# Two graph layers on one core: vectors by TensorE, four banks for the first preparation, later casts, chains cut at their bank, an earlier verdict

## The chip, the cores and the metric

The kernel runs on one core of a Trainium2 chip. Its time is the device time of the whole launch in microseconds (us). The engines of the core are called TensorE (PE in the profile; PEld is its weight load), VectorE (DVE), ScalarE (ACT), GpSimd (POOL) and SyncE (SP). Each executes its own stream of instructions in order, and they wait for each other through semaphores. Transfers between DRAM and on-chip memory are issued by SP, ACT or POOL.

## The reference

The input is x, 16 graphs (batches) of 1024 nodes with 256 features in float32, and adj, 16 matrices of 1024 x 1024 integers that are 0 or 1. Two layers follow each other. Layer 0 has 4 heads of 64 features and one edge type that occurs:

```python
h = einsum('bnd,hde->bhne', x, W)
e_src, e_dst = einsum('bhne,hte->bhtn', h, a_src), einsum('bhne,hte->bhtn', h, a_dst)
weight = where(adj == 0, -1e9, leaky_relu(mask * (e_src[i] + e_dst[j]), 0.01))
dst = softmax(weight) @ h + bias
out = norm_per_head(relu(dst) + h) * ln_gamma + ln_beta
x = layernorm(x + out)
```

Layer 1 is a transformer block with 8 heads of 32 features, whose queries, keys and values are all the normed input, and whose logits are masked by adj:

```python
normed = layer_norm(x, gamma1, beta1)
x1 = x + softmax(mask(q @ q.T / sqrt(32))) @ q        # q: normed, by heads
y = layer_norm(x1, gamma2, beta2)
x = layernorm(x + x1 + gelu(y @ W1 + b1) @ W2 + b2)
```

## The kernel before

`fast_path` holds the whole computation for the inputs that it assumes, and writes what it found about them into a small tile; `tile_two_graph_layers` makes one number, the verdict, from it, loads it into a register on all engines, and branches to a slow `general_path` where it is 0. With these inputs it is 1.

**Two streams in one program.** `layer0()` and `layer1()` are Python generators. Each yields after a piece of TensorE work, with the size of the piece and the tiles that the next one needs. A planner loop at the end of `fast_path` chooses which stream goes on. Layer 1 of batch b runs beside layer 0 of batch b+1. The planner keeps `place`, how far each stream is, and `COURSE`, which says how far layer 0 should be for each position of layer 1; `SLACK`, `SLACK1` and `STAY` say by how much the order may deviate, and `WORK0`, `WORK1` and `ATTN1` are the sizes of a batch in units of about 1 us of TensorE. The class `Pace` models the times that the engines need. The resulting order is the order of the instructions on TensorE, VectorE, ScalarE and GpSimd. SP is left to the framework, which may issue SP's transfers earlier than they are written.

**Chains.** Small work behind the matmuls (norms, residuals, copies) is a chain: a generator begun with `begin(chain, engine, *needs)` and driven on by `advance()` when the model finds its needs met. A chain is recorded as a user of the tiles that it needs or makes. When a buffer is to be reused, `settle` or `bank0` first runs its users to their end (`complete`), waits for other engines included.

**PSUM.** Of 8 banks, `ps_s` holds four (named ps: logits and hidden layer), `ps_o` two (po), and `ps_a` two (acc0 and acc1), handed out by `bank0` for layer 0 and for transposes.

**The front.** Layer 0's matrix W is loaded into `w0e` by eight transfers on ACT. `w0e` has eight more columns, W times a_src and a_dst for each head. For them a_src and a_dst are broadcast to all 128 partitions (four loads of 320 KB, two on SP and two on ACT), multiplied with W on VectorE and summed. `later_weights` is a chain that loads the vectors of the norms and the biases, and layer 1's w1 and w2 (1 MB each), on SP, and later folds gamma2 into w1 and beta2 into b1 (16 matmuls into po, w_sb<-w_sb,g_c on VectorE). `prepare` makes for each pair of 128-row blocks: xT (transposes through acc, copied by ScalarE), the projection acc<-w0e,xT, the exponentials dinv and v0 of the scores, hb (h), and `mask`. In batch 0 the mask comes from adjacency blocks ak, cast to bf16 by a POOL transfer and turned by TensorE; in later batches from adjb, a copy of adj cast to bf16 in DRAM (`cast_adj`, two POOL transfers a batch), read back through transposing transfers on SP (`load_adj`). `turn_sources` writes the exponentials of e_src to DRAM (esr<-rows), and `spread_factor` reads them back broadcast to all partitions (cb<-esr, 512 KB for each half of the rows and pair of heads; four groups a batch).

**Layer 0's attention** (`attention0`, 32 steps a batch) makes two weight tiles a step on VectorE (p<-cb,dinv,mask) three steps ahead, and multiplies them with v0 on TensorE (acc<-v,p). `residual0` and `after0` follow for each head or pair of heads: norm per head, sum with x (tile xl), layer 1's first norm, its transposed result nT for keys and queries (acc<-ident,sq, or ps), the values v1 and the input x1 of the residual. `handed` passes these to layer 1; when `half` asks for one that is not there, `finish_norms` completes the whole chains.

**Layer 1.** `attention1` has 32 steps a batch (half of the queries, four heads, block of 128 keys): four logits ps<-nT, their exponentials on ScalarE (p<-ps), the mask on VectorE (p<-p,mask), and the products into po in two shapes. Then `finish1` (residual and norm), and `mlp` in four chunks (ps<-yT,w_sb; gelu to hid on ScalarE; po<-w_sb,hid). `last_norm` adds the residual and writes zz and then out. `in_range` compares the collected sums (`seen`) of a batch with bounds and keeps the minimum in okr.

Of the kernel before, what the change touches and what calls it, by code (L numbers as in the profile page):

```python
# [39 lines left out]
P = 128  # L40
# [150 lines left out]
def fast_path(  # L191
# [19 lines left out]
    ok: bass.AP,  # L211
# [67 lines left out]

    w0e = const.tile([P, DC, D + 2 * H0], F32, name="w0e")  # L280
    for c in range(DC):
        for h in range(H0):
            nc.scalar.dma_start(w0e[:, c, h * HO : (h + 1) * HO], w0[h, c * P : (c + 1) * P, :])
# [4 lines left out]
    terms = ((a_src, nc.sync, w0e[:, :, D + H0 : D + 2 * H0]), (a_dst, nc.scalar, w0e[:, :, D : D + H0]))  # L288

    at = one.tile([P, 3, PAIR, HO, T], F32, name="v0")  # L290
    vectors = [at[:, i, :, :, :] for i in range(3)] + [one.tile([P, PAIR, HO, T], F32, name="xl")]
    for i, (src, queue, _) in enumerate(terms):
        for pair in range(H0 // PAIR):
            queue.dma_start(
                vectors[i * PAIR + pair].rearrange("p h e t -> p (h e t)"),
                bass.AP(
                    tensor=src.tensor,
                    offset=src.offset + pair * PAIR * HO * T,
                    ap=[[0, P], [1, PAIR * HO * T]],
                ),  # L300
            )

# [6 lines left out]
    for i, (_, _, dst) in enumerate(terms):  # L309
        for c in range(DC):  # L310
            t = two.tile([P, H0, HO], F32, name="z")
            for pair in range(H0 // PAIR):
                heads = slice(pair * PAIR, (pair + 1) * PAIR)
                nc.vector.tensor_mul(
                    t[:, heads, :],
                    w0e[:, c, pair * P : (pair + 1) * P].rearrange("p (h e) -> p h e", e=HO),
                    vectors[i * PAIR + pair][:, :, :, 0],
                )
            nc.vector.tensor_reduce(dst[:, c, :], t, axis=mybir.AxisListType.X, op=OP.add)
# [12 lines left out]
    def later_weights():  # L332
        for t, src in ((lng0_r, lng0), (lnb0_r, lnb0), (g1_r, gamma1), (be1_r, beta1), (b2_r, b2)):
            nc.sync.dma_start(t, bass.AP(tensor=src.tensor, offset=src.offset, ap=[[0, P], [1, D]]))
        for t, src in ((g1_c, gamma1), (be1_c, beta1), (g2_c, gamma2), (be2_c, beta2)):
            nc.sync.dma_start(t, src.rearrange("(c p) -> p c", p=P))
        nc.sync.dma_start(b1_sb, b1.rearrange("c p -> p c"))
# [4 lines left out]
        nc.sync.dma_start(w1_sb, w1.rearrange("(c p) f -> p c f", p=P))  # L342
        nc.sync.dma_start(w2_sb, w2.rearrange("(c p) d -> p c d", p=P))
# [16 lines left out]
        for c in range(DC):  # L360
            nc.vector.tensor_scalar(w1_sb[:, c, :], w1_sb[:, c, :], g2_c[:, c : c + 1], None, op0=OP.mult)
# [54 lines left out]
    def transpose_rows(dst, src, scale=None, shift=None):  # L416

        pt = side_bank([P, DC, GB, P])
# [74 lines left out]
    def load_x(t, b, k, count):  # L493
        nc.sync.dma_start(t, x[b, k * P : (k + count) * P, :].rearrange("(g p) d -> p g d", p=P))

    adj_blocks = {}
    x_blocks = {}
# [24 lines left out]
    def load_blocks(i):  # L522
        b, k = divmod(i, NB // GB)
        if b < B:
# [3 lines left out]
    def prepare(b, hb, esr, cbs, v0, dinv, mask):  # L528
# [4 lines left out]
        def turn_mask(k):  # L533
            i = b * NB + k
            pt = adj_blocks.pop(i)
            if b == 0:
                ak = pt
                pt, _ = bank0([P, NB, P], BF16)
# [15 lines left out]
            load_adj(i + 3)  # L554

        turning, scaling = [], []
        if b:
            cast_adj(b + 1)
        for k in range(0, NB, GB):
# [4 lines left out]
            transpose_rows(xT, xk)  # L564
            yield 0.45, bank0_ready, xT
            if b == 0:
                turn_mask(k)
                yield 0.0, bank0_ready, xT
# [4 lines left out]
            for g in range(GB):  # L573
# [4 lines left out]
                ph, bank = bank0([P, D + 2 * H0])  # L578
# [15 lines left out]
                yield 0.45, bank0_ready  # L594
                if g == 0 and b == 0:
                    if k == BPH:
                        cast_adj(1)
# [979 lines left out]
```

## Time and profile before

| What | us |
|---|---|
| median of 3 runs (lowest, highest) | 3255.43 (3252.06, 3255.72) |
| the profiled execution's own time | 3255.19 |
| its span, from first to last instruction | 3253.4 |
| TensorE busy | 3168.4 (97%) |
| VectorE busy | 2882.5 (89%) |
| ScalarE busy | 1961.9 (60%) |
| GpSimd busy | 511.3 (16%) |
| mean granted TensorE clock | 0.992 |

The profile is of one execution. An instruction's line tells the engine, the operation and its tiles as out<-in; numbers in the names are left out, so that a_src's vectors, v0 and v1 all read as "v", and w1, w2 as "w_sb". The operations are all recorded at one line of the file, the helper `Engine.call` (L61), so they are told apart by their tiles. A "q" behind an engine's name means its sequencer, which issues transfers and waits. "issue" in a chain is time for which the profile shows no wait. An idle time tells what ended it. Idle time of an engine that others do not wait for costs nothing.

### The profile page before, as it was taken

The numbers are of one execution on the slowest core, as the hardware profiler recorded it, in microseconds if no ns is written. First come the engines' busy times: TensorE is split into PE (matmuls) and PEld (weight loads), VectorE is DVE, ScalarE is ACT, GpSimd is POOL, SyncE is SP. The second block draws the span as 40 slices with busy tenths as digits, with TensorE's granted clock in tenths as the row PEclk, the third lists the DMA queues.
The fourth block names the chain that finished last, engine by engine and source line by source line (L and its number), as shares of the span: only waits on it lengthen the run. The fifth ranks groups of instructions, "written<-read, shape, count | busy, mean of one in ns | idle before, by whom it ended". The sixth has DMA issues, their size and how long they took to land.

```text
span 3253.4 us, 147229 instructions
## 1 busy us (share of the span) xinstructions
PE 3168.4 (97%) x67297; PEld 1979.3 (61%) x67297; DVE 2882.5 (89%) x4943; ACT 1961.9 (60%) x4256; POOL 511.3 (16%) x462
## 2 busy tenths in 40 slices
PE   5899999999999999999999999999999999999998
PEld 4557565575756657566575755757566575665745
DVE  5899898998989989898998989989898998989992
ACT  2473846748376583856738466483755838567483
POOL 1202112030110202112030120301102021120300
PEclk9799999999999999999999999999999999999999
DMA  7212202122031221303122031220312213011000
GB/s 169 58 38 59 63 26 67 39 63 52 26 85 21 70 46 32 87 20 73 36 66 56 26 74 33 63 52 25 87 26 68 41 42 80 20 44 21 30 7 16
DMA packets 209447, 163.18 MB, mean 50 GB/s; under 512 B 138480, under 2 KB 189680, under 8 KB 207856
## 3 DMA queue, kind: packets, MB, share of 16 engines
q1 hardware_dynamic: 204640, 119.07, 14.8%
q0 software_dynamic: 2592, 33.56, 5.3%
q8 instruction: 529, 8.67, 1.1%
q10 hardware_dynamic: 1584, 1.05, 0.1%
q14 instruction: 102, 0.84, 0.1%
HBM read 138.68 MB, written 48.50 MB: 58 GB/s over the span
## 4 chain that ended last, share of the span: by engine, by line
PE 75%; DVE 16%; ACT 4%; issue 3%; DMA 1%; POOL 0%; ACTq 0%; SPq 0%; POOLq 0%; DVEq 0%
PE po L61 28%; PE ps L61 28%; PE acc L61 19%; DVE p L61 14%; ACT p L61 2%; ACT o L61 0%; ACT nT L61 0%; DMA cb<-esr 0%; DVE o L61 0%; DVE st L61 0%; ACT zz L61 0%; DVE v L61 0%; DVE hb L61 0%; DVE z L61 0%; DVE relu L61 0%
## 5 line engine op out<-in xcount | busy, mean ns | idle before, releaser
L61 DVE TENSOR_TENSOR p<-p,mask 128x1024 f32<-128x1024 f32 x1024 | 1191.2, 1220 | 6.9 <-ACT p L61 6.9
L61 ACT ACTIVATE p<-ps 128x512 f32<-128x512 f32 x2006 | 1042.4, 612 | 235.9 <-PE ps L61 220.0
L61 DVE SCALAR_TENSOR_TENSOR p<-cb,dinv,mask 128x512 f32<-128x512 f32 x1024 | 709.3, 747 | 8.1 <-DMA cb<-esr 7.8
L61 PE MATMUL ps<-nT 32*128 32x512 f32 x4012 | 647.1, 641 | 2.2 <-ACT p L61 0.4
L61 ACT ACTIVATE hid<-ps,b_sb 128x256 f32<-128x256 f32 x512 | 242.0, 474 | 586.1 <-PE ps L61 586.1
L61 PE MATMUL acc<-v,p 128*64 128x65 f32 x16384 | 563.5, 225 | 31.0 <-DVE p L61 21.9
L61 PEld LDWEIGHTS po<-v,p 128*32 128x32 f32 x32768 | 397.3, 109 | 315.7 <-issue 264.6
L61 PEld LDWEIGHTS acc<-v,p 128*64 128x64 f32 x16384 | 536.7, 140 | 75.1 <-issue 14.4
L61 PE MATMUL po<-p,v 128*32 128x512 f32 x2048 | 543.4, 605 | 1.3 <-DVE p L61 1.3
L61 PE MATMUL po<-p,unit 128*32 128x512 f32 x2048 | 543.5, 605 | 0.0
L61 PE MATMUL po<-w_sb,hid 128*64 128x256 f32 x4096 | 476.2, 380 | 0.0
L61 PE MATMUL ps<-yT,w_sb 128*64 128x256 f32 x4096 | 475.7, 380 | 0.0
L61 POOL TENSOR_SCALAR r<-mv 128x4 f32<-128x4 f32 (+1 forms) x128 | 86.5, 676 | 2057.4 <-DVE mv L61 2019.5
L61 PE MATMUL po<-v,p 128*32 128x33 f32 x32768 | 393.1, 198 | 7.2 <-issue 6.7
L61 PEld LDWEIGHTS po<-w_sb,hid 128*64 128x64 f32 x4096 | 281.3, 137 | 146.3 <-issue 14.5
L61 PEld LDWEIGHTS ps<-yT,w_sb 128*64 128x64 f32 x4096 | 283.6, 137 | 135.4 <-issue 5.2
L61 POOL TENSOR_TENSOR r<-r,mhalf 128x8 f32<-128x8 f32 (+2 forms) x192 | 313.6, 1633 | 16.0
L61 PEld LDWEIGHTS ps<-nT 32*128 32x128 f32 x4012 | 201.9, 183 | 131.7 <-ACT p L61 84.5
L61 PEld LDWEIGHTS po<-p,v 128*32 128x32 f32 x2048 | 77.8, 108 | 321.7 <-issue 143.4
L61 DVE TENSOR_TENSOR z<-hb,bias_r 128x256 f32<-128x256 f32 x128 | 54.2, 423 | 163.8 <-ACT hb L61 163.8
L61 PE MATMUL acc<-w0e,xT 128*128 128x264 f32 x512 | 174.5, 435 | 10.5 <-issue 10.5
L61 ACT ACTIVATE mask<-ak,shift_c 128x1024 uint8<-128x1024 bf16 x120 | 142.1, 1184 | 0.0
(115 smaller groups left out, 2437.7 us busy)
## 6 DMA issues: line engine op xcount, KB each, us to landing
cb<-esr SPq DMA_DIRECT2D x64, 512.0 KB
adjb<-in_adj_dram POOLq DMA_DIRECT2D x30, 1024.0 KB, 11.5
xk<-in_x_dram SPq DMA_DIRECT2D x64, 256.0 KB
xl<-in_x_dram SPq DMA_DIRECT2D x32, 512.0 KB
out_dram<-zz SPq DMA_DIRECT2D x64, 256.0 KB
ak<-adjb SPq DMA_TRANSPOSE x240
ak<-in_adj_dram POOLq DMA_DIRECT2D x8, 256.0 KB, 6.8
w_sb<-in_L_gnn_W_dram SPq DMA_DIRECT2D x2, 1024.0 KB
```

Of the source, the lines that this page charges most:

```text
L61: return method(*args, **kwargs)
```

## The change

In the front:

- x's first block is the first transfer on SP. a_src and a_dst are loaded as one row of 5 KB each, on one partition. A matmul with a row of ones (taken from okr, which is set to 1) spreads each over 128 partitions in a ps bank, and VectorE multiplies whole 256-column rows of W with it. W comes in two transfers.
- `later_weights` issues its transfers on ACT instead of SP. The scaling of w1 by gamma2 goes from VectorE to ScalarE.
- batch 0's preparation takes its banks from the four of ps instead of the two of acc (`front_bank`).
- batch 1's casts are issued at the third step of batch 0's attention, no longer in its preparation, and its first three adjacency blocks are read at the 21st step.

In the rounds:

- `after0` ends with nT. The values (`values1`) and x1 with its ratio (`rows1`) are chains of their own; `half` completes only the chain that makes nT, and `values` asks for v1 when the products need it.
- `last_norm` ends with its sum out of po; the norm behind it is the chain `norm_rows`.
- b2 is added 70 instead of 60 us (in the model's time) after its half. `WORK0`, `SLACK1`, `STAY` and `COURSE` get other values.

At the end: the comparison of the last batch's sums, and a new `judge` that reduces everything to the verdict (with a transpose through a ps bank), stand ahead of the last chunk of the last batch's MLP. The steps behind the last norm that did so before, with an identity matrix of their own, go.

```diff
+    x_blocks = {0: two.tile([P, GB, D], F32, name="xk")}
+    load_x(x_blocks[0], 0, 0, GB)
+    terms = one.tile([P, H0, HO, T], F32, name="v0")
+    for i, src in enumerate((a_src, a_dst)):
+        nc.sync.dma_start(
+            terms[i * Q : i * Q + 1].rearrange("p h e t -> p (h e t)"),
+            bass.AP(tensor=src.tensor, offset=src.offset, ap=[[0, 1], [1, H0 * HO * T]]),
+        )
...
-        for h in range(H0):
-            nc.scalar.dma_start(w0e[:, c, h * HO : (h + 1) * HO], w0[h, c * P : (c + 1) * P, :])
+        nc.scalar.dma_start(
+            w0e[:, c, 0:D].rearrange("p (h e) -> p h e", e=HO),
+            w0[:, c * P : (c + 1) * P, :].rearrange("h p e -> p h e"),
+        )
...
+    for i, at in enumerate((D + H0, D)):
+        spread = ps_s.tile([P, D], F32, name="ps")
+        nc.tensor.matmul(
+            spread, okr[i * Q : i * Q + 1, 0:P], terms[i * Q : i * Q + 1, :, :, 0], start=True, stop=True
+        )
         for c in range(DC):
             t = two.tile([P, H0, HO], F32, name="z")
+            nc.vector.tensor_mul(t.rearrange("p h e -> p (h e)"), w0e[:, c, 0:D], spread)
+            nc.vector.tensor_reduce(w0e[:, c, at : at + H0], t, axis=mybir.AxisListType.X, op=OP.add)
...
-        nc.sync.dma_start(w1_sb, w1.rearrange("(c p) f -> p c f", p=P))
-        nc.sync.dma_start(w2_sb, w2.rearrange("(c p) d -> p c d", p=P))
+        nc.scalar.dma_start(w1_sb, w1.rearrange("(c p) f -> p c f", p=P))
+        nc.scalar.dma_start(w2_sb, w2.rearrange("(c p) d -> p c d", p=P))
...
-            nc.vector.tensor_scalar(w1_sb[:, c, :], w1_sb[:, c, :], g2_c[:, c : c + 1], None, op0=OP.mult)
+            nc.scalar.activation(w1_sb[:, c, :], w1_sb[:, c, :], AF.Copy, scale=g2_c[:, c : c + 1])
...
+    def front_bank(b, shape):
+        return bank0(shape) if b else (ps_s.tile(shape, F32, name="ps"), {})
...
-            load_adj(i + 3)
+            if b or k + 3 < NB:
+                load_adj(i + 3)
...
+            if b == 0 and i == 2:
+                cast_adj(1)
+            if b == 0 and i == 20:
+                for k in range(3):
+                    load_adj(NB + k)
...
-        yield "vector", normed
+        handed[b, n] = [None, None, nT]
+        norms[b, n, "values"] = values1(b, n, normed)
+        begin(norms[b, n, "values"], "vector", normed)
+        norms[b, n, "rows"] = rows1(b, n, normed, v2, r2, r3)
+        begin(norms[b, n, "rows"], "vector", normed, r3)
...
+    def values1(b, n, normed):
         v1 = two.tile([P, BPH, H1, HD + 1], F32, name="v1")
...
+        handed[b, n][1] = v1
+        yield from ()
+
+    def rows1(b, n, normed, v2, r2, r3):
         ratio = small.tile([P, BPH], F32, name="ratio")
...
+    def judge():
+
+        right = small.tile([P, NR], F32, name="seen")
+        nc.vector.tensor_scalar(right[:, : B * NB], types, N / 2 + 2.0, None, op0=OP.is_lt)
+        nc.vector.tensor_tensor(okr[:, : B * NB], okr[:, : B * NB], right[:, : B * NB], op=OP.min)
+        least = const.tile([P, 1], F32, name="least_r")
+        nc.vector.tensor_reduce(least, okr, axis=mybir.AxisListType.X, op=OP.min)
+        row = side_bank([1, P])
+        nc.tensor.transpose(row, least, ident)
+        nc.vector.tensor_reduce(least[0:1, :], row, axis=mybir.AxisListType.X, op=OP.min)
+        nc.vector.tensor_copy(verdict, least[0:1, :])
...
+            if b == B - 1 and (n, q) == chunks[-1]:
+                in_range(seen)
+                judge()
...
-        if g < GB - 1:
-            return
+        if g == GB - 1:
+            begin(norm_rows(b, k, z, mv), "vector", z)
...
-                    finish_norms(b, n)
+                    complete(norms[b, n, H0 - 1])
...
-    WORK0 = NB // GB * 2.25 + 2.0 + NB * H0 * 1.0
+    WORK0 = NB // GB * 2.0 + 2.0 + NB * H0 * 1.0
...
-    SLACK1 = 0.02
-    STAY = 0.017
-    COURSE = [(0.0, 1.0), (REST1 + 1.0, 1.0), (ATTN1, 1.31), (WORK1 - 12.0, 2.0), (WORK1, 2.0)]
+    SLACK1 = 0.03
+    STAY = 0.01
+    COURSE = [(0.0, 1.0), (REST1 + 1.0, 1.0), (ATTN1, 1.29), (WORK1 - 10.0, 2.0), (WORK1, 2.0)]
```

## The prediction

> **What bounds the kernel now.** I read the table of the engines first, then the kernel cut into windows, then the chain that ended last for both ends, then the waits and the order of time where the chain leaves TensorE (PE).
>
> ```profile
> PE 3168.4 (97%) x67297; PEld 1979.3 (61%) x67297; DVE 2882.5 (89%) x4943; ACT 1961.9 (60%) x4256; POOL 511.3 (16%) x462
> ```
>
> TensorE is busy for 3168.4 of 3253.4 us, so whoever moves nothing but waits can win 85 us at most. The windows (window: length, then busy PE, PEld, VectorE (DVE), ScalarE (ACT), POOL; granted clock; DMA share; GB/s) tell where these lie:
>
> ```profile
> 0.00:20.00 20.00, 1.94 (x12) 1.64 (x12) 3.61 (x16) 2.98 (x4) 3.10 (x10) 1.00 0.87 197
> 20.00:40.00 20.00, 16.23 (x105) 11.78 (x106) 7.42 (x19) 13.69 (x47) 3.12 (x6) 1.00 1.08 276
> 40.00:60.00 20.00, 10.01 (x227) 9.24 (x227) 11.09 (x20) 1.68 (x7) 0.00 (x0) 0.74 0.81 160
> 60.00:80.00 20.00, 14.39 (x349) 11.71 (x346) 19.79 (x36) 0.63 (x1) 1.93 (x2) 1.00 0.16 55
> ...
> 480.00:500.00 20.00, 20.00 (x392) 16.15 (x389) 19.69 (x46) 6.99 (x15) 3.89 (x4) 1.00 0.10 29
> ```
>
> Until 50 us no computing engine is full, while the 16 DMA engines nearly are (shares 0.87, 1.08, 0.81): the front waits for transfers. From 50 to 98 VectorE sets the pace (19.79 of 20), because batch 0's layer 0 runs with no layer 1 beside it. From 144 us on TensorE is full (20.00 of 20), with VectorE close behind (19.69). Over 200 to 3000 us all windows together show PE 2782 of 2800 busy. Layer 0's weights end at 120.7 in batch 0 and at 3072.7 in batch 15, so a round takes (3072.7 - 120.7)/15 = 196.8 us, of which about 1.3 are idle. So the two ends can be shortened, and the fifteen rounds between can hardly gain, but can lose fifteen times over.
>
> The chain of the front (start, length, what):
>
> ```profile
> 1.23 5.24 DMA v<-in_L_gnn_a_src_dram
> 6.47 0.02 issue
> 6.49 8.04 DMA w0e<-in_L_gnn_W_dram
> 14.53 0.02 issue
> 14.55 0.33 ACTq L61
> ...
> 20.89 4.66 PE acc L61 x16
> ...
> 32.16 3.78 DMA esr<-rows
> 35.94 0.02 issue
> 35.95 14.15 DMA cb<-esr
> 50.11 0.02 issue
> 50.13 1.47 DVE p L61 x3
> ```
>
> An old load holds a new one: ScalarE's queue cannot issue a load before an unrelated older one has landed, and ScalarE starts computing only at 14.9, behind its last issue. The first projection (20.89) waits for the columns made from a_dst, landed at 19.95. At the end the 14.15 us of cb stand alone: it shares the DMA engines with batch 1's two casts (issued at 33.3) and with w1 and w2 (2 MB, issued at 21.0).
>
> **The front, part by part.** (1) Vectors. Four broadcasts of 320 KB become two loads of 5 KB on one partition, behind x on SP: issues at 0.8, 1.2 and 1.7 (about 0.45 us each). The nearest row for their landing is esr<-rows, also small, 3.78 us: they are there at 5.9. W in two loads instead of eight, the same 256 KB: from 6 us (one issue and the latency of that row) to 14.5 (as now). The early transfers sum to about 2.2 MB by the profile's sizes (two x, W, three ak, bias, and 0.5 MB of xl, whose tile is now free at once); at the 197 to 276 GB/s of the rows that is 8 to 11 us, W is in the middle, I take 9.5. Then VectorE does four products of 128x256 and four reductions; three pairs follow the last half of W: 3 x (0.42 + 0.42) = 2.5 us, so the projection starts at 12.0 instead of 20.89. The product now reads PSUM. [...] here relu<-acc from PSUM takes 425 ns and hb<-hb,relu from SBUF 424, so I add nothing. The two spread matmuls (at most 0.44 us each, as acc<-w0e,xT with 264 columns) end before W lands.
>
> (2) Four PSUM banks instead of two for batch 0's preparation. From projection to second esr write: 32.16 - 20.89 = 11.3. ScalarE is busy 13.69 of the 16.8 us from 23.2 to 40, so the ping-pong costs at most 3 us over three to four blocks; I take 1.0 off the two blocks on the path (0 to 1.8): 22.3. esr lands as now, 3.8 later: 26.1.
>
> (3) cb without casts, w1 and w2. Bounds: 5 us (1 MB at the 211 GB/s of 0 to 60 us) and 14.15. Only the last ak blocks and x are beside it: 6.5, so the first p at 32.6. The rest of preparation ends at 12.0 + (42.3 - 20.9) - 2 = 31.4, inside. **Gain 50.1 - 32.6 = 17.5**, between 12 and 22. [...] But SP's order is free here (it issues w1 at 21 us, though it is written behind batch 0's preparation), while ScalarE's is the written one: the bytes leave the window. I take the row.
>
> What moves to later must hide. **Casts** (4 MB read) start after two steps of attention, about 36 us, and land within 12 us or so each (median 11.5); batch 1's masks are first made at 126.2, now about 109: 50 us of cover. They run beside the cb of group 2, whose buffer is free after eight steps and which is needed after sixteen; a step takes (98 - 50.1)/26 = 1.84 us there (52 p in that window, two to a step), so 15 us of cover against at most the 14 of now: I take 0, at most 3. **ScalarE's ten small loads** stand before the squares of the first head pair (10 x 0.35 us and waits for older landings); ScalarE is busy 0.63 of 20 us there. Behind them wait the squares, and for these VectorE; it takes the first (v0s) at 77.3 now, 27 us after its first p. w1 and w2 (issued at step 14, 32.6 + 14 x 1.84 = 58, some 10 us of transfer) are wanted by the matmuls that stand at 99.24 now, about 82 after. SP loses twelve issues. The three adjacency blocks queue their six transposing loads on SP at step 20, no longer ahead of esr; before, they blocked SP from 43.9 to 56.
>
> **Handoff to layer 1, 98 to 144.** VectorE, the pace-setter, loses the two scalings of w1 (1.41 us, to ScalarE, idle for 16.7 us there) from its path. The values, ratio and x1 of the first half (116.0 to 119.3, 3.3 us) stand before the last two p now; as own chains they may come later. I count half: 1.4 + 1.6 = **3.0 us**, between 0 and 5.
>
> **Rounds.** The course asks for 0.29 x 42 = 12.2 units of layer 0 by the end of attention 1, not 0.31 x 43 = 13.3. So about one step moves from attention 1 (where each insertion changes the array's shape) into the MLP phase (same 128x64 shape). Nearest price: the four logits of ps<-nT from a shape change take some 0.1 to 0.2 us longer than their work, so two half steps are 0.3 us; chains that stop at their bank and no longer hold VectorE for POOL (t<-r waits 23.5 us in all) can take some of the 1.3 idle. Against that, layer 0 ends two units later (about 1.6 us each by 76 us for 49 units). I take -0.27 a round, **4 us in 15 rounds**, from -15 to +10 in all.
>
> **Tail.** The last matmul ends at 3239.8, then:
>
> ```profile
> 3242.32 0.16 DVE t L61
> 3242.48 0.15 DVE right L61
> ...
> 3245.11 0.14 DVE verdict L1537
> ```
>
> After it all engines load the verdict (0.5 us) and branch; ScalarE is back 2.9 us after its branch, TensorE 4.6, and the span ends 2.9 us after TensorE. With the verdict long there, TensorE branches at 3240.3 and is back by 3245.0, ScalarE (last work to 3243.7) is back by 3247.1, and the end comes at 3250.0 to 3250.5: **3.0 us**, between 0 (if the last store sets the end) and 3.4. The price: in_range and judge (about 1.9 us of VectorE) now stand before a transpose ahead of the last chunk's matmuls on TensorE; VectorE is busy 4.5 of 20 us there but comes from a norm: 0 to 2.5, I take **0.6 lost**.
>
> Sum: 17.5 + 3.0 + 4.0 + 3.0 - 0.6 = 26.9 us. The profiled execution took 3255.2 (1.8 outside its span), the median is 3255.4: **3228 us**.
>
> **Rivals.** (A) The rounds gain too: the whole idle of 1.3 us and 0.3 of shape changes go, 15 x 1.6 = 24 instead of 4: 3208. For it: stalls by "DVE relu" and "DVE p" recur; against: TensorE and VectorE are both full. (B) The front gains little: cb stays slow ([...]7.7 us), and the casts and w1, w2 then collide with the second cb and ScalarE's queue (5 us): 3241. (C) Slower: the later end of layer 0. Each round's last norm chain then hands the second half's keys 3.2 us late, and the fifth step of attention 1 needs them: in round 2 the last p ends at 507.9, keys are stored from 530.9, the fifth logits start at 534.6. The slack is about 2.6 us there; planner's fillings may not cover it. If every round loses L, the end is 3232 + 15 L: it decides against the change above L = 1.6; at 2.2 it gives 3265. (D) The front's and the handoff's gain are given back in the VectorE stretch, where a load moved there (cb of group 2, or w1 for the matmuls at 99.24) comes that much late: 3228 + 20.5 + 3 = 3252.
>
> **Chances.** Main 0.60 (own range 3217 to 3239), A 0.12, B 0.16, C 0.07, D 0.05. Within 0.2% (6.5 us, about what a measurement of this kernel tells from no change) of 3255.4 fall most of D and a little of C: 0.04. Slower: 0.05. Faster: 0.91. The range from 3211 to 3246 leaves out C and D, and half of A at the lower end.
>
> **What the changed profile would show.** First projection near 12 and first p near 33 (wrong: above 40); cb landing in 5 to 8 us; attention windows still VectorE-full; last mask of batch 15 about 24 us earlier; a round between 196.2 and 197.2 (C: over 198.4, with TensorE waiting for nT or sq just after each MLP); 10.5 us from last matmul to end, not 13.6. A ScalarE queue that stands on its issues while VectorE waits for the squares would make the front's sum wrong.

## The result, and the profile after

The changed kernel takes 3212.38 us (median; 3207.75 to 3217.06), beside 3255.57 for the kernel before on the same chip (3252.06 to 3256.20): a ratio of 0.9868, 95% interval 0.9852 to 0.9883. The gain of 43 us is larger than the 27 forecast, inside the range (3211 to 3246) by 1.4 us, and it comes from other places than forecast. The profiled execution took 3212.37, its span is 3210.5 (before 3253.4).

From the page of the changed kernel, busy time, share of the span and instructions of each engine:

```profile
PE 3145.5 (98%) x67301; PEld 1966.0 (61%) x67301; DVE 2876.0 (90%) x4936; ACT 1964.8 (61%) x4258; POOL 498.0 (16%) x460
```

TensorE's busy time fell from 3168.4 to 3145.5 us, with practically the same number of matmuls. Over half of the gain was therefore counted as busy time before, and a bound of the rounds that is read from idle time misses it.

Where the 42.9 us of span lie can be read from four marks in both traces: the first weight tile p of batch 0, the first gelu (hid) of batch 0's MLP, the first gelu of batch 15's, and the end. (A "round" is the time from a batch's first gelu to the next one's. Where a mean round is given below, it is that of the fourteen from batch 0 to batch 14: 197.2 us before, 195.1 after. The fifteenth has no layer 0 beside it and takes 177.4 and 177.6.)

| stretch (us) | before | after | difference | forecast |
|---|---|---|---|---|
| start to first p | 50.1 | 39.3 | -10.8 | -17.5 |
| first p to first gelu of batch 0 | 195.8 | 197.0 | +1.2 | -3.0 |
| from there to first gelu of batch 15 (15 rounds) | 2938.7 | 2909.4 | -29.3 | -4.0 |
| from there to the end | 68.8 | 64.7 | -4.0 | -3.0 + 0.6 |

**The front.** The windows of the changed kernel (window: length, then busy PE, PEld, DVE, ACT, POOL; granted clock; DMA share; GB/s):

```profile
0.00:20.00 20.00, 12.26 (x78) 9.47 (x79) 7.36 (x24) 10.19 (x30) 5.37 (x15) 1.00 0.85 180
20.00:40.00 20.00, 6.20 (x47) 4.50 (x45) 4.17 (x10) 7.32 (x28) 0.80 (x2) 0.75 1.05 228
40.00:60.00 20.00, 16.40 (x398) 14.47 (x399) 19.83 (x35) 0.63 (x1) 0.00 (x0) 0.91 0.55 83
60.00:80.00 20.00, 14.96 (x336) 13.02 (x334) 19.76 (x36) 0.63 (x1) 2.62 (x2) 0.86 0.38 133
```

VectorE is full from 40 us on (before, its first weight tile came at 50.1). But between 20 and 40 the DMA engines are as full as before (1.05), and no computing engine is busy for more than 7.32 of the 20 us. The chain of the changed kernel says what they wait for:

```profile
1.45 8.44 DMA ak<-in_adj_dram
9.89 0.05 issue
9.94 2.92 PE ps L61 x12
...
20.81 8.73 DMA esr<-rows
29.54 0.02 issue
29.56 0.02 SPq L61
29.57 0.03 issue
29.61 9.71 DMA cb<-esr
39.31 0.02 issue
39.34 1.47 DVE p L61 x3
```

The compute part came as forecast or better: the second esr write is issued at 20.81 (forecast 22.3). The two transfers behind it did not: esr took 8.73 us instead of the 3.78 of before, cb 9.71 instead of 6.5. The order of time shows their company:

```profile
19.80 1.00 POOL L61 DMA_DIRECT2D adjb<-in_adj_dram  x2
...
20.81 0.50 SPq L61 DMA_DIRECT2D esr<-rows  x1
...
29.61 3.00 SPq L61 DMA_DIRECT2D cb<-esr  x2
...
34.98 5.47 SPq L61 DMA_TRANSPOSE ak<-adjb  x2
```

Batch 1's casts are written in the third step of attention, yet GpSimd issues them at 19.8 us, 13.5 us sooner than before (33.3). Nothing that they read or write depends on the attention, and the last instruction ahead of them on GpSimd, the last load of ak, is done by then.

**The rounds.** The kernel before, in order of time around the third step of batch 3's attention 1 (start, length, engine, operation, tiles, idle time before it and what ended it):

```profile
731.39 1.54 POOL L61 TENSOR_TENSOR r<-r,mhalf 128x2 f32<-128x2 f32 x1
...
731.53 1.18 PE L61 MATMUL ps<-nT 32*128 32x512 f32 x8
...
733.62 0.15 DVE L61 SCALAR_TENSOR_TENSOR t<-mv,r 128x2 f32<-128x2 f32 x1
...
733.86 1.10 ACT L61 ACTIVATE zz<-zz,t,r 128x256 f32<-128x256 f32 x2 [1.41 <-issue]
...
734.87 2.03 ACT L61 ACTIVATE p<-ps 128x512 f32<-128x512 f32 x4
...
735.50 2.57 PE L61 MATMUL ps<-nT 32*128 32x512 f32 x8
```

The logits of 731.53 are done by 732.71, but ScalarE stands until 733.86 in front of zz, the last step of last_norm. Zz needs t, and t needs r, which GpSimd finishes at 732.93; VectorE, busy with values (v<-sq,g_r), reaches t at 733.62. Only behind zz come the exponentials (734.87). The next logits need the banks that those exponentials empty, and take 2.57 us for eight matmuls instead of 1.18. The same step in the changed kernel:

```profile
721.29 1.54 POOL L61 TENSOR_TENSOR r<-r,mhalf 128x2 f32<-128x2 f32 x1
...
721.89 1.14 PE L61 MATMUL ps<-nT 32*128 32x512 f32 x8
722.00 1.02 ACT L61 ACTIVATE nT<-acc,be_c,g_c 128x256 f32<-128x256 f32 x2 [0.18 <-PE acc L61]
...
723.04 1.08 ACT L61 ACTIVATE p<-ps 128x512 f32<-128x512 f32 x2
```

Zz is no longer here, and the exponentials follow at once. The groups of zz on ScalarE over the whole execution, first before, then after (busy, mean ns of one, idle time in front of it):

```profile
L61 ACT ACTIVATE zz<-zz,t,r 128x256 f32<-128x256 f32 x128 | 70.2, 601 | 28.4 <-issue 28.0 <-ACT nT L61 0.4
```

```profile
L61 ACT ACTIVATE zz<-zz,t,r 128x256 f32<-128x256 f32 x128 | 69.9, 601 | 8.4 <-issue 8.2
```

ScalarE's standing time in front of zz falls by 20 us. That sum alone proves nothing: in run 1 it stays at 26.7 us and the rounds gain as much. What counts is whether exponentials stand behind zz. On TensorE, from one logits matmul to the next, a round takes 21.49 us before and 20.13 after, 1.36 x 14 = 19.0 us in the fourteen rounds. These lost 29.5 us in all, of which the windows book 21.9 as busy and 7.6 as idle time. A wait among logits is booked as busy because their rows overlap: each of the eight shows 0.6 to 0.7 us, and held ones start one or two every 0.48 us (735.50 to 737.48), where four start together when nothing holds them.

**The tail.** The verdict in the changed kernel (durations, then first and last start):

```profile
L61 DVE CAST verdict<-least_r x1: 143/143/143, 3180.7 to 3180.7; 1x1 int32<-1x1 f32 x1
L1558 PEldq TENSOR_LOAD <-verdict x1: 490/490/490, 3198.9 to 3198.9; - x1
L1558 POOLq TENSOR_LOAD <-verdict x1: 489/489/489, 3203.0 to 3203.0; - x1
```

It is made at 3180.7, where before it came at 3245.1. TensorE loads it at 3198.9, while its own queued matmuls run on to 3201.2. From the last matmul of the MLP to the end it is 9.3 us, before 13.6. What ends late in both kernels is GpSimd, whose long drain comes behind its branch (before, then after):

```profile
L1573 POOLq DRAIN  x3: 40/107/3173, 3249.4 to 3253.2; - x3
L1593 POOLq DRAIN  x3: 40/107/3173, 3206.5 to 3210.2; - x3
```

The other engines' last semaphores follow it. GpSimd loads the verdict 5.5 us behind the last matmul of the MLP before, and 1.8 us after.

### The profile page after: what moved, and what is told of

Read it like the earlier page. It is cut to its first block, busy times and chain, and to the rows that moved or that the text cites. A ratio compares the mean times of both kernels' runs of the same rounds, so it can differ in the third digit from the quotient of the medians.

```text
span 3210.5 us, 147003 instructions
## 1 busy us (share of the span) xinstructions
PE 3145.5 (98%) x67301; PEld 1966.0 (61%) x67301; DVE 2876.0 (90%) x4936; ACT 1964.8 (61%) x4258; POOL 498.0 (16%) x460
## 4 chain that ended last, share of the span: by engine, by line
PE 96%; DVE 2%; DMA 1%; issue 1%; ACT 0%; POOL 0%; POOLq 0%; SPq 0%
PE po L61 39%; PE ps L61 33%; PE acc L61 24%; DVE p L61 1%; DMA cb<-esr 0%; DVE hb L61 0%; DMA esr<-rows 0%; DMA ak<-in_adj_dram 0%; ACT mask L61 0%; DVE v0s L61 0%; DVE relu L61 0%; ACT sq L61 0%; ACT p L61 0%; ACT zz L61 0%; ACT nT L61 0%
## 5 line engine op out<-in xcount | busy, mean ns | idle before, releaser
L61 DVE SCALAR_TENSOR_TENSOR p<-cb,dinv,mask 128x512 f32<-128x512 f32 x1024 | 710.6, 746 | 10.5 <-DMA cb<-esr 10.5
L61 PE MATMUL ps<-nT 32*128 32x512 f32 x4012 | 628.3, 642 | 0.8 <-ACT p L61 0.8
L61 PEld LDWEIGHTS acc<-v,p 128*64 128x64 f32 x16384 | 549.7, 140 | 83.3 <-DVE p L61 26.2
L61 PE MATMUL acc<-v,p 128*64 128x65 f32 x16384 | 571.8, 225 | 27.3 <-DVE p L61 24.6
L61 PE MATMUL ps<-yT,w_sb 128*64 128x256 f32 x4096 | 484.8, 381 | 0.0
L61 POOL TENSOR_SCALAR r<-mv 128x4 f32<-128x4 f32 (+1 forms) x128 | 71.8, 561 | 2056.6 <-DVE mv L61 1853.1
L61 PEld LDWEIGHTS ps<-yT,w_sb 128*64 128x64 f32 x4096 | 276.8, 137 | 124.4 <-issue 8.0
L61 POOL TENSOR_TENSOR r<-r,mhalf 128x8 f32<-128x8 f32 (+2 forms) x192 | 281.1, 1464 | 16.0
L61 PEld LDWEIGHTS ps<-nT 32*128 32x128 f32 x4012 | 190.1, 184 | 128.4 <-ACT p L61 78.3
L61 PE MATMUL acc<-w0e,xT 128*128 128x264 f32 x480 | 167.0, 435 | 0.0
L61 POOL TENSOR_SCALAR r<-v0s 128x8 f32<-128x8 f32 x64 | 70.8, 1106 | 471.7 <-DVE v0s L61 470.4
```

Source lines behind the costliest of these rows:

```text
L61: return method(*args, **kwargs)
```

## The experiments

All marks are read from each kernel's trace as in the table above. "Before" stands for the kernel before in the same comparison: 3252.12 us for the first four kernels, 3253.71 for the next four, 3252.48 for three more, 3257.87 for the last. Runs of different comparisons are compared by their ratios to it; the changed kernel's is 0.9868. The executions of one kernel differ by 3 to 23 us, and a trace shows only one of them: those of run 1 and of "front and verdict alone" (9) are 5.6 us below their kernel's median, that of run 8 is 9 us above. A few microseconds between two traces are therefore not yet a difference between two kernels. My theory after the comparison of the traces: the last norm's cut carries the rounds, and the casts, issued too soon, held back the front.

**1. The last norm's cut alone, in the kernel before.**

```diff
-        if g < GB - 1:
-            return
-        statistics(z, mv, GB)
+        if g == GB - 1:
+            begin(norm_rows(b, k, z, mv), "vector", z)
+        yield from ()
+
+    def norm_rows(b, k, z, mv):
+        statistics(z, mv, GB)
```

> The kernel before with one edit: the last norm behind the second MLP product is a chain of its own (norm_rows), so that a new tile po completes only the sum out of the bank. My theory now: this edit made most of the 2.0 us that a round became shorter. In the kernel before ScalarE stands 1.41 us in front of zz in each round, at the third step of attention 1, with the exponentials queued behind it, and the next four logits take 2.57 us instead of 1.14. Expected: that wait gone, a round 1.3 to 1.5 us shorter (195.7 instead of 197.1), the whole 3235 us (3230 to 3242). Rival (the planner's new values made the rounds shorter): no change, 3250 to 3258, and the 1.41 us still there.

3228.53 us (3222.95 to 3231.03), ratio 0.993 [0.9913, 0.9946], 23.6 us less than before and below the expected range. From first gelu of batch 0 to that of batch 15 it takes 2909.5 us against 2938.7: -29.2 by a trace that flatters it, about the whole of the rounds' gain; by the median the greater part of it. On TensorE the time from one logits matmul to the next falls by 1.89 us a round. The same place of batch 3's attention, and the group of zz:

```profile
726.67 2.07 ACT L61 ACTIVATE p<-ps 128x512 f32<-128x512 f32 x4 [0.25 <-PE ps L61]
...
728.60 1.11 ACT L61 ACTIVATE zz<-zz,t,r 128x256 f32<-128x256 f32 x2
...
728.86 1.14 PE L61 MATMUL ps<-nT 32*128 32x512 f32 x8
```

```profile
L61 ACT ACTIVATE zz<-zz,t,r 128x256 f32<-128x256 f32 x128 | 70.2, 604 | 26.7 <-DVE t L61 18.5 <-issue 8.2
```

Here zz stands behind the exponentials, and the logits take 1.14 us. Yet ScalarE waits in front of zz for 26.7 us in all, nearly as long as before: in each of the fifteen rounds the wait has moved to the MLP, where ScalarE stands idle for some 3 us behind zz as well. So the wait is not gone, as was expected; it is out of the exponentials' way.

**2. The changed kernel without this cut.** The diff of 1, reversed.

> The changed kernel with the last norm in one chain again (norm_rows undone). Theory: the wait of 1.4 us in front of zz is back in each round, 1.3 to 1.5 us a round, 3232 us (3226 to 3240). Rival (planner's values): stays at 3212, within 4 us.

3255.98 us (3247.96 to 3267.75), ratio 1.0016 [1.0007, 1.0025]. Both expectations missed: undoing the cut takes all 43 us back, where making it had won 24. Runs 8 to 11 look for the difference.

**3. The casts truly later, in the changed kernel.** A GpSimd instruction that reads a weight tile stands ahead of them.

```diff
             if b == 0 and i == 2:
+                hold = small.tile([P, 1], F32, name="hold")
+                nc.gpsimd.tensor_scalar(hold, p[:, 0, 0:1], 1.0, None, op0=OP.mult)
                 cast_adj(1)
```

> The changed kernel in which the two casts of batch 1 really come later: a GpSimd instruction that reads one column of a weight tile of the second step stands in front of them, so that GpSimd, which had nothing to wait for and issued them at 19.8 us, issues them after the first weights. Theory: the esr write (8.73 us to its landing) and the cb loads (9.71) were slow because the casts shared the DMA engines. Expected: esr 4 to 5 us, cb 5 to 7 us, first weights at 31 to 33 instead of 39.3, whole 3205 us (3202 to 3208). The transposing loads of adjb come later and hold the next cb on SP until about 52 us; it is wanted at about 61. Rival (the two landings are slow for another reason, such as the last adjacency blocks, x and xl, or the writing to DRAM itself): first weights stay at 37 to 40, time 3210 to 3215 or slower by late transposes.

3209.65 us (3207.79 to 3211.81), ratio 0.9871 [0.9855, 0.9888]. In order of time:

```profile
21.10 0.50 SPq L61 DMA_DIRECT2D esr<-rows  x1
...
24.76 0.90 SPq L61 DMA_DIRECT2D cb<-esr  x2
...
28.63 9.36 DVE L61 SCALAR_TENSOR_TENSOR p<-cb,dinv,mask 128x512 f32<-128x512 f32 x14 [0.25 <-DMA cb<-esr]
...
31.43 1.08 POOL L61 DMA_DIRECT2D adjb<-in_adj_dram  x2
...
42.25 11.75 SPq L61 DMA_TRANSPOSE ak<-adjb  x6
...
54.11 1.03 SPq L61 DMA_DIRECT2D cb<-esr  x2
62.32 1.42 DVE L61 SCALAR_TENSOR_TENSOR p<-cb,dinv,mask 128x512 f32<-128x512 f32 x2 [7.83 <-DMA cb<-esr]
```

With the casts out of the way esr lands in 3.60 us and cb in 3.85 (8.73 and 9.71 beside them). The first weight tile starts at 28.63, 10.7 us sooner than in the changed kernel. So the casts were the cause of the slow landings. But the time missed the theory: by its ratio the kernel is no faster than the changed one (0.9868). The six transposing reads of batch 1, written at step 20, now stand on SP from 42.25 to 54.0, and cb of the third group queues behind them. VectorE waits 7.83 us for it, and the last weight tile of batch 0 ends at 106.8 instead of 109.4. Most of the transfers' gain went into SP's queue.

**4. The early verdict alone, in the kernel before.**

```diff
             complete(halves[n][2])
+            if b == B - 1 and (n, q) == chunks[-1]:
+                in_range(seen)
+                judge()
...
-            in_range(seen)
+            if b < B - 1:
+                in_range(seen)
```

(and the old steps behind the last norm removed, as in the change)

> The kernel before with the verdict made ahead of the last chunk of the last MLP, and nothing else. Theory: the branch comes behind the last work of each engine and TensorE's own branch runs beside its last matmuls, so the tail from the last matmul to the end falls from 13.6 to about 9.5 us: 3251.5 us (3250 to 3253), and no wait of TensorE ahead of the transpose of the row. Rival (the transpose waits for VectorE): a gap of 1 to 2.5 us of TensorE about 14 us before its end, 3253 to 3255.

3246.67 us (3243.69 to 3254.67), ratio 0.9985 [0.9977, 0.9992], 5.4 us less than before and below the theory's range. The trace has 65.0 us from batch 15's first gelu to the end, before 68.8, so 3.8 us of the gain are in the tail. No wait of TensorE stands at judge's transpose, so its forecast price of 0.6 was nothing.

**5. The transposing reads later as well.** A small VectorE write of step 20 into their tiles keeps them behind it, so that SP passes both loads of cb first.

```diff
             if b == 0 and i == 20:
                 for k in range(3):
-                    load_adj(NB + k)
+                    load_adj(NB + k, True)
...
+            if late:
+                nc.vector.memset(ak.rearrange("p (e q) -> p e q", q=HALF)[:, :, 0:1], 0.0)
```

> The changed kernel with the casts held behind a weight tile (as in the run before this one) and, new, batch 1's six transposing reads held behind a small VectorE write of step 20, so that SP passes the cb loads of groups 2 and 3 first. Theory (what ate the gain of the held casts was SP's queue: cb of group 2 stood 11.75 us behind the transposing reads, and VectorE waited 7.8 us for it): the wait at 62 us goes, the last weight tile of batch 0 ends near 99 us instead of 106.8, and the time is 3202 (3198 to 3206). Rival (VectorE's stretch is held by something else next, such as w1 and w2 or the squares on ScalarE): the last weight tile still ends at 105 to 109 us, and the time is 3208 to 3213.

3201.27 us (3197.67 to 3202.49), ratio 0.9835 [0.9818, 0.9851]: the fastest kernel of this study, and the theory's number. In order of time:

```profile
40.44 14.52 SPq L61 DMA_DIRECT2D cb<-esr  x2
...
53.16 2.73 DVE L61 SCALAR_TENSOR_TENSOR p<-cb,dinv,mask 128x512 f32<-128x512 f32 x4
...
69.04 8.30 SPq L61 DMA_TRANSPOSE ak<-adjb  x6
```

The first load of cb leaves at 40.44, the transposes at 69.04, and no p waits. The last weight tile of batch 0 ends at 97.5 (changed kernel 109.4), and the first gelu of batch 0 comes at 226.6 (236.4). A round is as in the changed kernel, 195.1. Together with run 3 this shows both causes in the front: the casts beside esr and cb, and the transposing reads ahead of cb on SP.

**6. The planner's values of before, in the changed kernel.**

```diff
-    WORK0 = NB // GB * 2.0 + 2.0 + NB * H0 * 1.0
+    WORK0 = NB // GB * 2.25 + 2.0 + NB * H0 * 1.0
...
-    SLACK1 = 0.03
-    STAY = 0.01
-    COURSE = [(0.0, 1.0), (REST1 + 1.0, 1.0), (ATTN1, 1.29), (WORK1 - 10.0, 2.0), (WORK1, 2.0)]
+    SLACK1 = 0.02
+    STAY = 0.017
+    COURSE = [(0.0, 1.0), (REST1 + 1.0, 1.0), (ATTN1, 1.31), (WORK1 - 12.0, 2.0), (WORK1, 2.0)]
```

The 70 us of b2 go back to 60 with them.

> The changed kernel with the planner's values (WORK0, SLACK1, STAY, COURSE, the 70 us of b2) of before. Theory (the rounds' gain is the last norm's chain alone): the time stays within 3 us of the changed kernel's, 3209 to 3215, a round within 0.2 us of 195.1. Rival (the prediction's reason: a step less in attention 1, and layer 0 two units later, worth 0.27 us a round, or a multiple of it): 3216 to 3230, a round of 195.4 to 196.3.

3212.11 us (3208.60 to 3214.91), ratio 0.9874 [0.9857, 0.9890], against 3212.38 (0.9868): the theory. A round takes 195.2 us.

**7. The cut of after0 undone, in the changed kernel.**

```diff
+        yield "vector", normed
         handed[b, n] = [None, None, nT]
-        norms[b, n, "values"] = values1(b, n, normed)
-        begin(norms[b, n, "values"], "vector", normed)
-        norms[b, n, "rows"] = rows1(b, n, normed, v2, r2, r3)
-        begin(norms[b, n, "rows"], "vector", normed, r3)
-
-    def values1(b, n, normed):
```

> The changed kernel with the values and x1 put back into the chain that makes nT (the cut of after0 undone), the last norm's cut kept. Theory (the last norm's cut carries the rounds): no more than 0.2 us a round and 1.6 us of the handoff come back, 3212 to 3217. Rival (the cut of after0 carries the wait of TensorE in front of acc<-v,p, which is 0.9 us a round shorter in the changed kernel): 3222 to 3228, a round near 196.0.

3219.84 us (3218.96 to 3221.77), ratio 0.9896 [0.9880, 0.9913]: 7.5 us more, between the two expectations. A round takes 195.7 us, 0.6 more than in the changed kernel, and the logits account for it: from one to the next 20.83 us a round, against 20.13. The wait in front of acc<-v,p that the rival named did not come back.

**8. Both cuts undone, in the changed kernel** (diffs of 2 and 7).

> The changed kernel with both cuts undone, the last norm's and that of after0. Undoing the last norm's alone cost 43 us, 2.9 us a round, where making it alone in the kernel before won 24. Theory (the values as a chain of their own are what makes the uncut last norm dearer: they are driven on at the same place, and VectorE does them between the norm's steps while ScalarE stands in front of zz): a round falls back to that of before, 197.1, and the time to 3240 to 3245. Rival (the planner's values or the front make it dearer): a round stays at 198, and the time at 3252 to 3258.

3256.68 us (3245.61 to 3268.29), ratio 1.0010 [1.0001, 1.0019]. The theory falls: under the new values of the planner it is not the values' chain that makes the uncut norm dear.

**9 to 11. What makes the uncut last norm dear.** Front and verdict alone (diffs of 2, 6 and 7 on the changed kernel); the changed kernel without the last norm's cut and with the planner's values of before (diffs of 2 and 6); and the planner's new values alone in the kernel before.

> The front and the early verdict alone: the changed kernel with both cuts (last norm, after0) undone and the planner's values of before. By the trace of the changed kernel the front's first weight tile comes 10.8 us sooner and the tail is 4.3 us shorter (5.4 in the run of the verdict alone). Theory (the planner's new values are what made the uncut last norm dearer in the two runs without its cut): a round is back at 197.1, no idle second in the middle of attention 1, and the time is 3237 (3234 to 3241). Rival (something of the front makes it dearer, such as the scaling of w1 or the loads on ScalarE): a round stays at 198, and the time at 3250 to 3258.

> The changed kernel with the last norm's cut undone and the planner's values of before; the cut of after0 stays. Theory (the planner's values make the uncut last norm dearer): a round of 196.6 to 197.2, 3230 to 3239. Rival (they don't): 3250 to 3258, a round of 198.

> The kernel before with only the planner's values changed (WORK0, SLACK1, STAY, COURSE, the 70 us of b2). Theory (with the last norm uncut, these values put its completion where TensorE has nothing beside it): a round of 198.0, 0.9 more than before, 3262 to 3268. Rival 1 (the prediction's term: 0.27 us a round saved): 3248 to 3251. Rival 2 (they do nothing): 3252 to 3256.

| kernel | last norm | after0 | planner's values | ratio | a round | idle before logits | lost at half clock |
|---|---|---|---|---|---|---|---|
| before | whole | whole | old | 1 | 197.2 | 1.8 | 0 |
| 9, front and verdict alone | whole | whole | old | 0.9971 | 197.3 | 1.8 | 0 |
| 10, with the cut of after0 | whole | cut | old | 0.9997 | 197.9 | 6.9 | 3.4 |
| 8 | whole | whole | new | 1.0010 | 198.6 | 14.4 | 22.2 |
| 2 | whole | cut | new | 1.0016 | 198.0 | 14.4 | 13.7 |
| 11, the values alone | whole | whole | new | 1.0051 | 198.1 | 14.5 | 13.7 |
| changed, 1, 6 and 7 | cut | either | either | 0.9868 to 0.993 | 195.1 to 195.7 | 0 | 0 |

(us; the last two columns are sums from first gelu of batch 0 to that of batch 15: TensorE's idle time in front of ps<-nT, and half the time for which its granted clock was 0.5.)

Front and verdict alone: 3242.90 us (3237.32 to 3247.57), ratio 0.9971 [0.9961, 0.9981], 2 us over the theory's range, with its round. Without the last norm's cut and with the old values: 3252.03 (3243.08 to 3256.73), ratio 0.9997 [0.9988, 1.0006]: the rival's time and round. The new values alone: 3270.38 (3266.62 to 3273.04), ratio 1.0051 [1.0034, 1.0067], 18 us slower than before and over the theory's range.

So two things make the whole last norm dear, and they do not add up. The new values do (9 against 8: 13 us by the ratios; alone: 18 us), though they are worth nothing in the changed kernel. Under the old values the cut of after0 does, too (9 against 10: 9 us); there ScalarE stands 33.6 us in front of zz instead of 28.4. The kernel with the values alone, in order of time:

```profile
1331.83 1.09 ACT L61 ACTIVATE zz<-zz,t,r 128x256 f32<-128x256 f32 x2 [1.29 <-issue]
...
1332.83 1.00 ACT L61 ACTIVATE nT<-acc,be_c,g_c 128x256 f32<-128x256 f32 x2
...
1333.73 4.00 ACT L61 ACTIVATE p<-ps 128x512 f32<-128x512 f32 x8
1334.37 2.58 PE L61 MATMUL ps<-nT 32*128 32x512 f32 x8 [1.02 <-ACT p L61]
1336.88 0.93 PE L61 MATMUL po<-p,v 128*32 128x512 f32 x1
```

and the windows around it, in the columns of above:

```profile
1333.00:1336.90 3.90, 2.88 (x48) 1.42 (x39) 3.83 (x9) 3.90 (x9) 0.00 (x0) 1.00 0.19 67
1337.00:1340.40 3.40, 3.40 (x74) 1.74 (x71) 2.62 (x3) 0.73 (x2) 0.00 (x0) 0.51 0.02 5
1340.40:1343.80 3.40, 3.40 (x86) 1.79 (x86) 2.45 (x4) 2.60 (x8) 0.00 (x0) 0.99 0.00 0
```

With these values zz falls where nT's copies also stand ahead of the exponentials on ScalarE. TensorE has no projection of layer 0 between the two logits there, as it had at 734.20 before, and is idle for 1.02 us. A stretch of 3.4 us follows in which its granted clock is halved (0.51), and so about 1.7 us are lost, an estimate that takes TensorE as the bound there. In this kernel such stretches sum to 27.3 us, or 13.7 us of work; its rounds are 12.5 us longer than before in all. For run 2 that closes the sum: from first gelu of batch 0 to that of batch 15 it is 40.7 us longer than the changed kernel, of which 13.7 are the clock, and 27.0 about what the cut was worth (run 1: 29.2). In run 10 the same sum leaves 34.8 us, about 5 of which are its longer idle time before the logits. The executions agree: of run 2's seventeen the slowest (3267.75 us) has the lowest mean clock, 0.981, the fastest (3247.96 us) 0.988.

Not every idle microsecond is followed by a slow stretch: run 2 has one of about 1.03 us in nearly every round, and seven stretches. The stretches last 3.413 us in the trace's clock record, or twice that, and their starts lie on a raster of it: 1337.0, 1535.0 and 1733.0 us in the kernel with the values alone, 198.0 apart, which is 58 times 3.413.

**12. What is left with only front, late reads, verdict and the last norm's cut** (run 5 with the diffs of 6 and 7).

> The front with the held casts and the later transposing reads, the early verdict and the last norm's cut; the cut of after0 undone and the planner's values of before. Theory (with the last norm cut, neither the cut of after0 nor the planner's values is worth anything in the rounds, and in the handoff they cost): from the run of front and verdict alone, whose first gelu of batch 0 is at 231.4 us against 236.4 in the changed kernel, the 11 us of the later reads, the 2909.5 us from first gelu of batch 0 to that of batch 15 that the last norm's cut alone gave, and the changed kernel's 64.7 us from there to the end: 3196 to 3197 (3193 to 3200). Rival (the cut of after0 and the values go with the last norm's cut: undoing both costs the 7.5 us that undoing the first alone cost): 3206 to 3212, a round of 195.6.

3207.57 us (3204.42 to 3208.18), ratio 0.9842 [0.9826, 0.9859]; by its ratio as good as run 5 (0.9835), by its trace 6.7 us longer in its span. The theory missed in both its terms: the first gelu of batch 0 came at 227.1 (4.3 us before that of front and verdict alone, not 11), and the fifteen rounds took 2914.7 us, not 2909.5. Both terms came from traces 5.6 us below their kernels' medians; 3196.5 + 2 x 5.6 = 3207.7, an estimate that would explain the miss, though no trace tells where in an execution these 5.6 us lie. Whether the cut of after0 and the values help beside the late reads is not settled by this run.

## Why the prediction was right and wrong

**Direction and range held, but the sum did so by errors of opposite sign.** By the trace the parts are -10.8, +1.2, -29.3 and -4.0, where -17.5, -3.0, -4.0 and -2.4 stood. That the range held is luck: with the front and the handoff as forecast (10.9 us more) the rounds would have carried the time to about 3201, below the range. Of the signs that the prediction named, three did not come: cb in 5 to 8 us (9.71), a round of 196.2 to 197.2 (195.0 by its mark, the last weight tiles) and 10.5 us of tail (9.3).

**Front, step (1) and (2): right in size, (1) on another path.** The projection starts at 10.8 us by the trace (forecast 12.0), but not behind W's columns, which are done at 8.9: it stands behind transposes that wait for the first ak until 9.9, a path that the prediction did not count. The products out of PSUM took 0.41 to 0.42 us each, so adding nothing for them was right. The second esr write is issued at 20.81 (22.3).

**Front, step (3): the failed step is "Casts ... start after two steps of attention, about 36 us".** They started at 19.8. The position in the program was taken for a time. On SP the prediction had seen that a transfer is issued ahead of its place (w1 at 21 us), but it did not ask what keeps GpSimd, which has almost nothing to do in this stretch (0.80 of the 20 us from 20 on), from reaching the casts at once. The terms that followed, esr in 3.8 us and cb in 6.5, were right or too high for the case that was meant: run 3 has 3.60 and 3.85. That "the bytes leave the window" held for w1 and w2 (issued at 58.9 us), not for the casts. With cb at its 14.15 us of before, the front would have been put at 9.8 (an estimate: 17.5 less 14.15 - 6.5), and 10.8 came, partly by luck: esr and cb took 8.73 and 9.71 us, where 3.8 and 14.15 would have stood.

**"SP loses twelve issues ... The three adjacency blocks queue their six transposing loads on SP at step 20": wrong in time, too.** By its own 1.84 us a step they would come near 69 us. They stood on SP at 35 to 46 us in the changed kernel, and in run 3, from 42 to 54 us, they cost VectorE 7.83 us. This is the mechanism of rival D (cb of group 2 late), in a place where I had taken 0, at most 3.

**Handoff, 3.0: not there, and open.** From first p to first gelu of batch 0 the changed kernel takes 197.0 us against 195.8. Front and verdict alone take 192.3, but in their fastest execution. Runs 7 and 8, which differ only in the last norm and execute the same instructions up to this mark, take 195.9 and 199.4. So these traces cannot tell whether the 3 us exist and what took them; that w1's scaling now lies on ScalarE (2.19 us for both halves, at 95.49) is all that they show.

**Rounds, 4.0: the failed step is the bound, "of which about 1.3 are idle. So ... the fifteen rounds between can hardly gain".** It was read from TensorE's busy rows, and these hide a wait inside a group of matmuls. The last norm's cut alone took 29.2 us out of fifteen rounds by its trace (23.6 us of the whole by medians), 1.95 a round, more than all the idle time. A row that points there was in the profile before: zz on ScalarE, 28.0 us of standing in front of it. Only the order of time shows what these cost, because run 1 keeps 26.7 of them and loses nothing by it. The prediction looked at "t<-r waits 23.5 us in all" and named the right cause, chains that hold an engine for GpSimd, but capped it at the 1.3 us. Rival A had 24 us for the rounds and a chance of 0.12; on this term it was the nearer one in size, though it counted on idle time, which gave only 7.6 us. The step of layer 0 that moves by the planner's values, which the -0.27 was built on, is worth nothing in the changed kernel (run 6). Nor is the price of a change of the array's shape shown: in the kernel before, of the eight logits at 731.53 the first four last 692 ns and the other four 587, but the eight at 735.50, which wait for their banks with no other shape between them, show the same two times. The cut of after0 is worth 7 to 9 us beside the last norm's (run 7).

**Rival C** (later end of layer 0, over 198.4 us a round) did not happen, as the rounds of 195.1 show. The kernels that keep the last norm whole under the new values come near its figure (198.0 to 198.6) in another way: an idle microsecond, then a halved clock (with the values alone 1.02 us, then 3.4 us at 0.51).

**Tail, 3.0 and -0.6: right in kind, short in size.** 4.0 by the trace. The prediction read that the end comes 2.9 us after TensorE. But TensorE is through its branch at 3203.0, 7.5 us before the end, because its sequencer did not wait for its last matmuls; the end follows GpSimd's branch and drain, which start earlier by 3.7 us against the last matmul. And the price of judge was zero.

## What to carry to other kernels

Read the bound of a stage from start to start of one kind of matmul over a round: a "busy" TensorE row can contain the wait (here 21.9 of 29.5 us). The standing time of the engine that feeds it tells where to look, and the order of time there tells whether anything needed stands behind. To delay a transfer, give it something to wait for; its place in the program delayed nothing on an engine that had no other work (the casts left at 19.8 us by their place, at 31.43 behind the read of a weight tile). Then ask what the moved transfer now stands in front of. Cut a chain where it would make one engine wait for another, because what it costs depends on what stands behind it, and a later change of the order can raise that price (the last norm's cut was worth 24 us in the kernel before, 43 in the changed one).

## What the runs showed of the hardware that was not expected

- **An idle time of 1.02 us on TensorE can be followed by 3.4 us at half clock** (the kernel with the values alone: idle up to 1334.37 us, granted clock 0.51 from 1337.0 to 1340.4). TensorE's row was busy for 2.88 of the 3.90 us ahead of the slow stretch. Its work was less, since 2.58 us of that are eight logits that take 1.14 us where nothing holds them. The kernel before has such stretches ahead of its first round: its granted clock is 0.50 from 86.42 to 89.83, 93.25 to 96.66 and 100.08 to 110.32 us (one, one and three times 3.413 us), and in the 3.4 us ahead of each TensorE was busy for 1.62, 0.90 and 2.44 us. No run here shows from which share on it happens.
- **Two transfers that VectorE waits for, esr and cb, landed in 3.60 and 3.85 us with the casts held (run 3), and in 8.73 and 9.71 beside them.**
- **TensorE's sequencer loads the verdict 2.3 us before the end of its own last matmuls** (3198.9 against 3201.2).
